# A graph layer's row gathers: one tile in 88 fetched by SP row by row, in place of a GpSimd gather

## The chip, the cores and the metric

The kernel runs on one core of a Trainium2 chip. A core has TensorE (matmuls, "PE" in the profile, its weight loads "PEld"), VectorE ("DVE"), ScalarE ("ACT"), GpSimd ("POOL") and SyncE ("SP"), an on-chip memory of 128 partitions (SBUF), accumulators for TensorE (PSUM), and DMA engines that move data between the chip's main memory and SBUF. SP here only issues transfers. Times are device microseconds of one launch; the number compared is the median of several launches.

## What is computed

A layer of a graph network, all in float32: 12,500 nodes with 96 features, 412,500 edges sorted by target node, 4 features an edge.

```
node    = mlp(x, W_node)                        # mlp: relu(h @ W + b), then a batch norm over the rows
edge    = mlp(edge_attr, W_edge)
message = mlp([x[src], x[dst], edge], W_msg)    # 412,500 rows
agg     = segment_sum(message, dst)
out     = layernorm(x + agg + node)
```

The product with W_msg is split by its three parts. `x @ W_msg[0]` and `x @ W_msg[1]` are made once for all nodes and stand in main memory as the tables `p_tab` and `q_tab`. For an edge the kernel then needs the row `src` of `p_tab` and the row `dst` of `q_tab`. Since edges are sorted by `dst`, rows of `q_tab` come as short windows; rows of `p_tab` lie anywhere and have to be gathered, 384 bytes each.

## The kernel before

A tile is 128 edges, a group (`GT`) four tiles, a block (`BG`) four groups. There are 806 groups in 202 blocks. `gather` (L162) fetches one group of `p_tab` rows by four indirect transfers on GpSimd, one for each tile: the edge numbers in `src` choose the row that lands on each of 128 partitions.

The first 26 blocks ("early", the constant `SPILL`) are gathered while the tables, the node part and the edges' statistics are still being computed, and are parked in main memory (`spill`). Gathers of later groups go to a ring of 25 slots in SBUF (`RING`, tile `pg`), which is filled before the long stage starts. In the long stage (L502 to L534) one step k handles one group. Steps run over the late blocks with the early ones spread evenly among them. For each step:

- at the first group of a block, `load(s + 2)` has SP fetch the edge features (L396) and the edges' relative targets (L397) for two blocks at once, then read the block's first target into a register (L400) and fetch the window of `q_tab` with that address (L405); `fetch(s + 1)` has SP read a parked block back (L412);
- `linear(k + 1)` has TensorE compute z, the target and edge part of the next group (L452);
- `message(k)` has VectorE add z and the gathered rows (`hs`, L467) and ScalarE apply relu (L469). This addition is the last reader of the ring slot;
- `sums(k - 2)` has TensorE multiply the messages by the 0/1 matrix of their targets and by themselves (L484), for the sums and for the statistics; `edges` (L437), `prepare` (L444, L445) and `add` (L497, L498) serve whole blocks;
- if the step's group was a late one, `ahead_of(ahead)` takes the slot just freed and gathers the group 25 places further on.

The order of instructions on all five engines in this stage is the order written (`manual_schedule`); waits between engines are put in by the framework. Each engine works its list in order, so an SP instruction that waits holds back everything SP issues after it. Landings of SP's transfers are counted on a few counters that take turns; a transfer waits until the one before it on the same counter has landed.

Of the kernel before, what the change touches and what calls it, by code (L numbers as in the profile page):

```python
# [11 lines left out]
F32 = mybir.dt.float32  # L12
I32 = mybir.dt.int32
# [3 lines left out]
ET = mybir.EngineType  # L17
# [3 lines left out]
N, C, E, ED = 12500, 96, 412500, 4  # L21
EPS = 1e-5
P = 128
# [3 lines left out]
GT, GE, BG = 4, 512, 4  # L27
NT = -(-E // P)
NG = -(-NT // GT)
NBL = -(-NG // BG)  # L30
NTP, NGP = NBL * BG * GT, NBL * BG
EP = NGP * GE
# [21 lines left out]
KR = C + WN + 1  # L54

SPILL = 26 * BG
RING = 25
RAW = 3
SKEW = 6
HB, RB = 2, 3  # L60
CL, CE = 2, 2
J = 8


# [12 lines left out]
def gnn(ctx, tc, t):  # L77
    nc = tc.nc
    const = ctx.enter_context(tc.tile_pool(name="const", bufs=1))
    dram = ctx.enter_context(tc.tile_pool(name="dram", bufs=1, space=DRAM))  # L80
    p_tab = dram.tile([NN, C], F32, name="p_tab")
# [10 lines left out]
    nc.sync.dma_start(src_raw, t["src"][:, :RAW * BG * GT])  # L92
    ring = rpool.enter_context(tc.tile_pool(name="ring", bufs=RING))
    xp = xpool.enter_context(tc.tile_pool(name="x", bufs=1)).tile([C, XW], F32, name="xp")
# [64 lines left out]
            queues[c // CH % len(queues)].dma_start(rows[:, c:c + CH, :], r)  # L159
            yield  # L160

    def gather(g, pg):  # L162
        tab, idx = (t["x"], src_raw) if g < RAW * BG else (p_tab, src)
        for i in range(min(GT, NT - g * GT)):
            k = g * GT + i
            nc.gpsimd.indirect_dma_start(  # L166
                out=pg[:, i, :], out_offset=None, in_=tab[:, :],
                in_offset=bass.IndirectOffsetOnAxis(ap=idx[:, k:k + 1], axis=0))
        return pg
# [107 lines left out]
    def edge_norm():  # L277

        with tc.tile_pool(name="es", bufs=2) as work, tc.tile_pool(name="es1", bufs=1) as one, \
                tc.tile_pool(name="es_ps", bufs=4, space=PSUM) as ps:  # L280
            stats = one.tile([P, NS, NBL, 6], F32, name="estats")
            for b in range(NBL):
                if b % J == 0:
                    yield
                    ea = work.tile([P, J, GE], F32, name="ea")
                    n = min(J, NBL - b)
                    for i in range(NS):
                        nc.sync.dma_start(ea[Q * i:Q * i + 2 * EK, :n, :],
                                          t["ea"][EK * i:EK * (i + 2), b:b + n, :])
                for i in range(NS):  # L290
                    k = NS * b + i
                    if k % 2 == 0:
                        pr = ps.tile([P, 2, GE], F32, name="pr")
                    nc.tensor.matmul(pr[:, k % 2, :], wide[Q * i:Q * i + 2 * EK, :],  # L294
                                     ea[Q * i:Q * i + 2 * EK, b % J, :], start=True, stop=True)
                    if k % 2:
# [32 lines left out]
            nc.vector.tensor_scalar(w_e, w_msg[:, 2, :], a_e, None, op0=OP.mult)  # L329

    def fast(ring):
        def ahead_of(g):
            return gather(g, ring.tile([P, GT, C], F32, name="pg"))

        with tc.manual_schedule(engines={ET.SP, ET.Pool}):
            with tc.tile_pool(name="tab_w", bufs=1) as work, tc.tile_pool(name="tab_ps", bufs=2, space=PSUM) as ps:
# [18 lines left out]
            for _ in store:  # L355
                pass
            got = {g: ahead_of(g) for g in range(SPILL, SPILL + RING)}

# [10 lines left out]
        with tc.tile_pool(name="fix", bufs=1) as fix, tc.tile_pool(name="msg", bufs=2) as work, \  # L369
# [17 lines left out]
            def load(s):  # L387

                b = order[s]
                first = SPILL // BG  # L390
                c, o = ((b - first) // CL * CL + first, CL) if b >= first else (b // CE * CE, CE)
                if c not in eas:
                    o = min(o, NBL - c)
                    eas[c] = work.tile([P, o, GE], F32, name="ea" if b >= first else "eae")
                    for i in range(BG):
                        nc.sync.dma_start(eas[c][Q * i:Q * i + EK, :, :], t["ea"][EK * i:EK * (i + 1), c:c + o, :])  # L396
                    nc.sync.dma_start(eas[c][EK:P:Q, :, :], rel_d[:, c * BG * GE:(c + o) * BG * GE]  # L397
                                      .rearrange("o (b g e) -> (o g) b e", g=BG, e=GE))
                ea = eas[c][:, b - c, :]
                _, val = nc.values_load_multi_w_load_instructions(  # L400
                    base[:, b:b + 1], engines=[ET.SP], min_val=0, max_val=N - 1,
                    skip_runtime_bounds_check_because="they are nodes' numbers")
                rows = q_tab[bass.ds(val[0], WN), :]
                rows = bass.AP(rows.tensor, rows.offset, [[C, WN], [WS * C, BG], [1, C]], None, rows.runtime_checks)
                nc.sync.dma_start(rhs[C:C + WN, s % RB, :, :], rows)  # L405
                block[s] = ea

            def fetch(s):
                b = order[s]
                if b * BG < SPILL:  # L410
                    back = work.tile([P, BG, GT, C], F32, name="pb")
                    nc.sync.dma_start(back, spill[b].rearrange("p g (a c) -> p g a c", a=GT))  # L412
                    for i in range(BG):
                        got[b * BG + i] = back[:, i, :, :]
# [18 lines left out]
            def edges(s):  # L433

                prs[s] = ps.tile([P, BG, GE], F32, name="pr", bufs=1)
                for i in range(min(BG, NG - order[s] * BG)):
                    nc.tensor.matmul(prs[s][:C + WN, i, :], we[Q * i:Q * i + EK + 1, :],  # L437
                                     block[s][Q * i:Q * i + EK + 1, :], start=True, stop=True)

            def prepare(s):  # L440

                n = min(BG, NG - order[s] * BG)
                pr, x = prs[s], left[s % 2]
                nc.scalar.activation(x[:C, :n, :], pr[:C, :n, :], AF.Relu)  # L444
                nc.vector.tensor_scalar(x[C:C + WN, :n, :], pr[C:C + WN, :n, :], 0.0, None, op0=OP.is_equal)  # L445

            def linear(k):
                s, g = steps[k]
                n = min(GT, NT - g * GT)
                zs[k] = ps.tile([P, GT, C], F32, name="z")  # L450
                for i in range(n):
                    nc.tensor.matmul(zs[k][:, i, :], left[s % 2][:KR, g % BG, i * P:(i + 1) * P],  # L452
                                     rhs[:KR, s % RB, g % BG, :], start=True, stop=True)

            def message(k):
                s, g = steps[k]
                n = min(GT, NT - g * GT)
                i = g % BG
                h, z, pg = hb[s % HB], zs.pop(k), got.pop(g)
                if i == 0:  # L460
                    nc.vector.tensor_tensor(  # L461
                        h[:, :, :, C + 1:C + 1 + WN], rel[:, g:g + BG, :].unsqueeze(3).to_broadcast([P, BG, GT, WN]),
                        iota.unsqueeze(2).to_broadcast([P, BG, GT, WN]), op=OP.is_equal)
                if i % 2 == 0:
                    pair[0] = work.tile([P, 2, GT, C], F32, name="hs")
                hs = pair[0]
                nc.vector.tensor_add(hs[:, i % 2, :n, :], z[:, :n, :], pg[:, :n, :])  # L467
                if i % 2 and n == GT:
                    nc.scalar.activation(h[:, i - 1:i + 1, :, :C], hs, AF.Relu)  # L469
                elif i % 2 or g == NG - 1:  # L470
                    for o in range(i // 2 * 2, i + 1):
                        m = GT if o < i else n
                        nc.scalar.activation(h[:, o, :m, :C], hs[:, o % 2, :m, :], AF.Relu)
# [13 lines left out]
            def add(s):  # L487
# [9 lines left out]
                    nc.vector.tensor_tensor(to, pa[:, i:n:2, C + 1:C + 1 + WN], to, op=OP.add)  # L497
                nc.vector.tensor_add(gram[:, :n, :], pa[:, :n, :C + 1], gram[:, :n, :])  # L498

            n, ahead = len(steps), SPILL + RING  # L502
            with tc.manual_schedule(engines={ET.SP, ET.Pool, ET.PE, ET.DVE, ET.Activation}):
                load(0)
                fetch(0)
                load(1)
                edges(0)
                prepare(0)
                linear(0)
                for k in range(n + SKEW):  # L510
                    s, g = steps[min(k, n - 1)]
                    if k < n and g % BG == 0:
                        if s + 2 < len(order):
                            load(s + 2)
                        if s + 1 < len(order):
                            fetch(s + 1)
                    if k + 1 < n:
                        linear(k + 1)
                    if k < n:
                        message(k)  # L520
                    if 0 <= k - 2 < n:
                        sums(k - 2)
                    if k < n and s + 1 < len(order):
                        if g % BG == 0:
                            edges(s + 1)
                        if g % BG == 2:
                            prepare(s + 1)
                        if g % BG == 3 and order[s + 1] < RAW:
                            convert(s + 1)
                    if k >= SKEW and (k - SKEW) % BG == 0:  # L530
                        add((k - SKEW) // BG)
                    if k < n and g >= SPILL and ahead < NG:
                        got[ahead] = ahead_of(ahead)
                        ahead += 1  # L534

            d = fix.tile([C, BG, C], F32, name="d")
            s = fix.tile([C, 3], F32, name="s")
# [237 lines left out]
```

## Time and profile before

| | |
|---|---|
| median of 3 launches | 5365.1 us (5362.86 to 5375.22) |
| the profiled execution's own time | 5383.6 us |
| its span, first to last instruction | 5381.9 us |
| busy in the span: TensorE, VectorE, ScalarE, GpSimd | 3389.5, 1708.3, 1077.3, 3088.7 us |
| mean granted TensorE clock | 0.662 of full |
| gathers on GpSimd into the ring | 2807, mean 958 ns |
| main memory traffic | 50 GB/s over the span |

A row of instructions gives the source line, the engine, what is written and read, the count, the busy time, the mean duration of one, and then the engine's idle time just before these instructions and what ended most of it. "issue" there means that the profile shows no wait, "remote" that it can't name who ended the wait. A row of waits gives who waited for whom, the total in us, the number of times and the longest. SPq rows are SP's own list: its durations are those of issuing.

### The profile page before, as it was taken

What the parts mean: (1) busy time and instruction counts of PE and PEld (TensorE: products, weight loads), DVE (VectorE), ACT (ScalarE), POOL (GpSimd) and SP (SyncE); (2) the same over time, 40 slices, a digit from 0 to 9 for tenths busy, and PEclk for the clock granted to TensorE, in tenths of its full rate; (3) what the DMA queues carried; (4) which work ended last, traced back from release to release, by engine and by line L of the source; (5) the groups of instructions that cost most, each with busy time, mean ns of one, the idle gap of its engine ahead of it and who ended that gap; (6) DMA issues with size and microseconds to landing.
All of it is one profiled execution on the core that took longest, in us unless ns stands there. A gap on an engine that the chain in (4) does not pass through costs nothing. (4 is left out here: it accounts for less than half of the span.)

```text
span 5381.9 us, 46696 instructions
## 1 busy us (share of the span) xinstructions
PE 3389.5 (63%) x16705; PEld 2576.6 (48%) x16705; DVE 1708.3 (32%) x2635; ACT 1077.3 (20%) x1015; POOL 3088.7 (57%) x3231
## 2 busy tenths in 40 slices
PE   5557653566666666666666666666666666765668
PEld 5423321354545555445554445454555544554557
DVE  1446542622222222223222223222232223222225
ACT  0235432311111111111111111111111111111112
POOL 5553455255566666666666665666666666666660
PEclk9755555566766666666676676666666666667667
DMA  5333322111111111111111111111111111111112
GB/s 165 127 87 66 71 62 50 27 37 33 39 44 37 43 43 43 44 37 43 43 43 41 45 36 43 43 42 44 37 43 42 42 45 36 43 43 42 45 36 83
DMA packets 154401, 270.78 MB, mean 50 GB/s; under 512 B 83463, under 2 KB 83976, under 8 KB 153154
## 3 DMA queue, kind: packets, MB, share of 16 engines
q0 software_dynamic: 103136, 158.62, 13.8%
q1 hardware_dynamic: 47936, 98.39, 6.4%
q10 hardware_dynamic: 3088, 10.71, 0.6%
q8 instruction: 133, 2.18, 0.2%
q14 instruction: 108, 0.88, 0.1%
HBM read 225.88 MB, written 41.60 MB: 50 GB/s over the span
## 5 line engine op out<-in xcount | busy, mean ns | idle before, releaser
L166 POOL DMA_INDIRECT pg<-p_tab,src x2807 | 2689.2, 958 | 1785.6 <-DVE hs L467 953.3
L452 PE MATMUL z<-rhs,left 128*128 128x96 f32 x6446 | 1221.4, 337 | 886.4 <-issue 766.5
L452 PEld LDWEIGHTS z<-rhs,left 128*128 128x128 f32 x6446 | 1094.8, 248 | 1181.1 <-issue 987.6
L484 PE MATMUL pa<-h 128*97 128x128 f32 x6446 | 1241.8, 331 | 522.8 <-issue 519.7
L484 PEld LDWEIGHTS pa<-h 128*97 128x97 f32 x6446 | 1012.0, 209 | 628.3 <-issue 626.2
L467 DVE TENSOR_TENSOR hs<-z,pg 128x384 f32<-128x384 f32 x702 | 384.7, 555 | 2634.4 <-remote 1730.7
L469 ACT ACTIVATE h<-hs 128x768 f32<-128x768 f32 x402 | 339.7, 845 | 2891.3 <-DVE hs L467 1768.6
L294 PE MATMUL pr<-ea,wide 10*128 10x512 f32 x1212 | 403.1, 1074 | 296.3 <-issue 197.6
L166 POOL DMA_INDIRECT stage<-p_tab,src x368 | 352.9, 959 | 355.8 <-DMA spill<-stage 224.6
L437 PE MATMUL pr<-ea,we 6*127 6x512 f32 x1404 | 458.7, 856 | 80.9 <-issue 67.9
L444 ACT ACTIVATE left<-pr 96x2048 f32<-96x2048 f32 x202 | 377.2, 1867 | 641.5 <-remote 452.0
L445 DVE TENSOR_SCALAR left<-pr 31x2048 f32<-31x2048 f32 x202 | 462.8, 2291 | 130.7 <-ACT left L444 84.2
L300 DVE BATCH_NORM_STATS2 estats<-r 128x6 f32<-128x512 f32 x606 | 365.5, 701 | 333.9 <-issue 217.8
L294 PEld LDWEIGHTS pr<-ea,wide 10*128 10x128 f32 x1212 | 203.3, 321 | 494.8 <-issue 316.3
L298 ACT ACTIVATE r<-pr 128x1024 f32<-128x1024 f32 x303 | 296.3, 1026 | 459.2 <-remote 261.4
L437 PEld LDWEIGHTS pr<-ea,we 6*127 6x127 f32 x1404 | 133.4, 235 | 255.1 <-issue 241.8
L461 DVE TENSOR_TENSOR h<-rel,iota 128x496 f32<-128x496 f32 x202 | 134.8, 667 | 0.0
L154 PE MATMUL pt<-w_msg,xp 96*128 96x96 f32 x392 | 89.3, 422 | 61.8 <-issue 38.5
L497 DVE TENSOR_TENSOR agg<-pa,agg 97x62 f32 x404 | 90.1, 223 | 105.0 <-remote 78.8
L154 PEld LDWEIGHTS pt<-w_msg,xp 96*128 96x128 f32 x392 | 85.5, 330 | 65.4 <-issue 50.6
L467 DVE TENSOR_TENSOR hs<-z,pb 128x384 f32<-128x384 f32 x104 | 57.2, 554 | 177.7 <-PE z L452 82.4
L498 DVE TENSOR_TENSOR gram<-pa,gram 97x388 f32<-97x388 f32 x202 | 111.4, 551 | 0.0
(107 smaller groups left out, 611.5 us busy)
## 6 DMA issues: line engine op xcount, KB each, us to landing
pg<-p_tab,src POOLq DMA_INDIRECT x2807
spill<-stage SPq DMA_DIRECT2D x26, 768.0 KB
pb<-spill SPq DMA_DIRECT2D x26, 768.0 KB
ea<-in_ea SPq DMA_DIRECT2D x75, 160.0 KB
rhs<-q_tab SPq DMA_DIRECT2D x202, 46.5 KB
ea<-in_ea SPq DMA_DIRECT2D x352, 20.0 KB
stage<-p_tab,src POOLq DMA_INDIRECT x368
q_tab<-trow SPq DMA_DIRECT2D x7, 672.0 KB
```

The costliest lines, as they stand in the source:

```text
L154: nc.tensor.matmul(pt[:, g, :], xp[:, k:k + P], w, start=True, stop=True)
L166: nc.gpsimd.indirect_dma_start(out=pg[:, i, :], out_offset=None, in_=tab[:, :], in_offset=bass.IndirectOffsetOnAxis(ap=idx[:, k:k + 1], ax ...
L294: nc.tensor.matmul(pr[:, k % 2, :], wide[Q * i:Q * i + 2 * EK, :], ea[Q * i:Q * i + 2 * EK, b % J, :], start=True, stop=True)
L298: nc.scalar.activation(r, pr, AF.Relu)
L300: nc.vector.bn_stats(stats[:, (k - o) % NS, (k - o) // NS, :], r[:, 1 - o, :])
L437: nc.tensor.matmul(prs[s][:C + WN, i, :], we[Q * i:Q * i + EK + 1, :], block[s][Q * i:Q * i + EK + 1, :], start=True, stop=True)
L444: nc.scalar.activation(x[:C, :n, :], pr[:C, :n, :], AF.Relu)
L445: nc.vector.tensor_scalar(x[C:C + WN, :n, :], pr[C:C + WN, :n, :], 0.0, None, op0=OP.is_equal)
L452: nc.tensor.matmul(zs[k][:, i, :], left[s % 2][:KR, g % BG, i * P:(i + 1) * P], rhs[:KR, s % RB, g % BG, :], start=True, stop=True)
L467: nc.vector.tensor_add(hs[:, i % 2, :n, :], z[:, :n, :], pg[:, :n, :])
L469: nc.scalar.activation(h[:, i - 1:i + 1, :, :C], hs, AF.Relu)
L484: nc.tensor.matmul(pas[s][:, g % BG, :C + 1 + WN], h[:r, i, :C + 1], h[:r, i, :C + 1 + WN], start=i == 0, stop=i == n - 1)
```

## The change

The ring has 24 slots. Of every 22 groups (`SG`) that are gathered ahead in the long stage, one is marked `by_row`: GpSimd gathers three of its four tiles, and SP fetches the fourth, one row at a time. A list of its 128 row numbers (a new input, `rows`) is brought into one partition by one small transfer, 22 groups earlier. At every second group (`SS`) SP loads twelve (`SR`) of these numbers into registers and issues twelve transfers of one row each, from `p_tab` at the register's address to one partition of the slot. Eleven such batches make the tile. A group is marked if at least 22 groups are left from it on.

```diff
-RING = 25
+RING = 24
+SR, SS = 12, 2
+SG = SS * -(-P // SR)
...
-    def gather(g, pg):
+    def gather(g, pg, without=0):
         tab, idx = (t["x"], src_raw) if g < RAW * BG else (p_tab, src)
-        for i in range(min(GT, NT - g * GT)):
+        for i in range(min(GT, NT - g * GT) - without):
...
+            def row_numbers(g):
+                lin = work.tile([1, P], I32, name="lin")
+                nc.sync.dma_start(lin, t["rows"][g * GT + GT - 1:g * GT + GT, :])
+                return lin
+
+            def rows_of(pg, lin, lo, hi):
+                _, val = nc.values_load_multi_w_load_instructions(
+                    lin[:, lo:hi], engines=[ET.SP], min_val=0, max_val=N - 1,
+                    skip_runtime_bounds_check_because="they are nodes' numbers")
+                for p in range(lo, hi):
+                    nc.sync.dma_start(pg[p:p + 1, GT - 1, :], p_tab[bass.ds(val[p - lo], 1), :])
...
             n, ahead = len(steps), SPILL + RING
+            lins = {ahead: row_numbers(ahead)}
...
                     if k < n and g >= SPILL and ahead < NG:
-                        got[ahead] = ahead_of(ahead)
+                        m = (ahead - SPILL - RING) % SG
+                        if m == 0:
+                            by_row = ahead if ahead + SG <= NG else None
+                        got[ahead] = ahead_of(ahead, int(ahead == by_row))
+                        if by_row is not None and m % SS == 0:
+                            if m == 0 and ahead + 2 * SG <= NG:
+                                lins[ahead + SG] = row_numbers(ahead + SG)
+                            lo = m // SS * SR
+                            rows_of(got[by_row], lins[by_row], lo, min(lo + SR, P))
                         ahead += 1
```

`ahead_of` passes `without` on to `gather`.

More of the change, by code (lines that the diff above doesn't have):

```diff
@@ L331, in fast, with ahead_of @@
     def fast(ring):
-        def ahead_of(g):
-            return gather(g, ring.tile([P, GT, C], F32, name="pg"))
+        def ahead_of(g, without=0):
+            return gather(g, ring.tile([P, GT, C], F32, name="pg"), without)
         with tc.manual_schedule(engines={ET.SP, ET.Pool}):
@@ L749 @@
     give("src", np.pad(s, (0, EP - E)).reshape(NTP, P).T)
+    give("rows", np.pad(s, (0, EP - E)).reshape(NTP, P))
     give("dst", d.reshape(NTP, P).T)
```

## The prediction

> **What bounds the kernel now.** I read the groups of instructions first, then the waits of GpSimd and of SP, then the order of time inside the long stage (from 1033 us, where the gathers go on, to 5250 us, where the last one ends).
>
> ```profile
> span 5381.9 us, 46696 instructions
> L166 POOL DMA_INDIRECT pg<-p_tab,src x2807 | 2689.2, 958 | 1785.6 <-DVE hs L467 953.3
> L452 PE MATMUL z<-rhs,left 128*128 128x96 f32 x6446 | 1221.4, 337 | 886.4 <-issue 766.5
> L467 DVE TENSOR_TENSOR hs<-z,pg 128x384 f32<-128x384 f32 x702 | 384.7, 555 | 2634.4 <-remote 1730.7
> ```
>
> No engine is full. One gather costs 0.95 us and 0.30 us to the next, 1.25 us in all, 5.0 us for a group of four. GpSimd's waits:
>
> ```profile
> POOL pg L166 <- DVE hs L467: 953.3, 175, 132.5
> POOL pg L166 <- issue: 785.0, 2477, 3.0
> ```
>
> It gathers in bursts, and each burst ends when the ring has no free slot, until an addition on L467 frees one. In the gather records of the stage I count 157 waits of 1 to 6 us (564 us, 3.6 each), 25 longer ones (286 us, where groups from the spill are consumed) and 3367 us of gathering: together 4217 us for 677 groups, 6.23 us a group; a burst has 4.3 groups. So the stage is the time of the gathers plus a gap after each burst. Why the ring runs out shows in order of time (start, length, engine, count, idle before):
>
> ```profile
> 3020.01 0.56 DVE L467 TENSOR_TENSOR hs<-z,pg 128x384 f32<-128x384 f32 x1 [6.86 <-PE pr L437]
> ...
> 3024.93 1.03 PE L452 MATMUL z<-rhs,left 128*128 128x96 f32 x3 [1.08 <-issue]
> 3029.28 0.94 POOL L166 DMA_INDIRECT pg<-p_tab,src  x1 [0.30 <-issue]
> ...
> 3033.44 1.02 DVE L467 TENSOR_TENSOR hs<-z,pg 128x384 f32<-128x384 f32 x2 [12.87 <-remote]
> 3034.15 1.92 PE L452 MATMUL z<-rhs,left 128*128 128x96 f32 x8
> 3034.27 0.94 POOL L166 DMA_INDIRECT pg<-p_tab,src  x1 [4.04 <-DVE hs L467]
> ```
>
> From 3016 to 3033 TensorE advances by about one instruction in 0.70 us, waiting for nothing shown; three microseconds after GpSimd stops it does eight in 1.9 us again. I call this the slow mode. Ten to fifteen microseconds after a burst begins it sets in, and it ends with the burst: I find 1545 us of it in the stage, 2.28 us a group. Three windows of 3.6 us, two slow and one fast (columns: TensorE busy and its instructions, weight loads and theirs, and so on):
>
> ```profile
> 2139.00:2142.60 3.60, 0.76 (x3) 0.48 (x3) 0.00 (x0) 0.00 (x0) 2.84 (x3) 0.50 0.23 52
> 3050.80:3054.40 3.60, 0.73 (x4) 0.71 (x4) 0.00 (x0) 0.82 (x1) 2.84 (x3) 0.71 0.19 41
> 3128.00:3131.60 3.60, 3.60 (x33) 2.79 (x31) 1.92 (x4) 1.69 (x2) 1.66 (x2) 1.00 0.14 37
> ```
>
> SP is hit too, which matters here: in the first of them, its register instructions on L405 took 697 and 709 ns; outside the slow mode they take 37, 17 and 29. VectorE's stay at 50 to 100 ns in both.
>
> **The change part by part.** *Removed from GpSimd:* one gather in 88. The first by-row group is 128, the last one must leave 22 groups behind it, so there are 30; 30 x 1.25 = 37 us, which lies in bursts and so on the path. *Ring 24 for 25:* one group less is gathered ahead of the stage (5 us more inside it) and one less is left after the last gather (85 us for about 25 groups, 3.4 us less): 2 us. The lead of a gather over its use, about 140 us, falls by 6, and hides the rest.
>
> *Added to SP:* 30 x 128 = 3840 transfers of 384 B, each with an address calculation and a register move before it, 330 loads of row numbers, 30 loads of a list. The trace has these instructions:
>
> ```profile
> L377 SPq DMA_DIRECT2D rhs<-bias x12: 581/589/609, 1012.5 to 1019.5; - x12
> L405 SPq FUSED_REGOPS  x202: 3/37/707, 1022.9 to 5284.3; - x101
> L405 SPq MOVE rhs<-q_tab x202: 2/29/1387, 1023.0 to 5284.4; - x101
> L405 SPq DMA_DIRECT2D rhs<-q_tab x202: 258/290/780, 1023.0 to 5292.7; - x101
> ```
>
> L377 is the nearest row: one partition, 384 B, 0.63 us from one to the next. With 0.09 and 0.06 for the two register instructions a row costs 0.78 us; by the issue of L405 (31 partitions, 0.34 from one to the next) it would be 0.49. I take 0.78, as the one-partition transfer is the same shape. Here the Trainium skill's rule can be weighed ("DMA: Bandwidth & Descriptors", section "Latency and other measured facts"): a tiny transfer can't be faster than about 0.8 us. Over SP's eight landing counters, which each row transfer must find free, that would be an estimated 0.1 us a row, 13 us a tile: hidden, and the sum would be the bare 35 us gained. By the row of the trace SP's own issue is what counts: 128 x 0.78 = 100 us a tile. The same page's section "Issuing engines are not separate DMA queues" says that issuing from more engines saves only the sequencer's time, usually small; here that time (1.25 us a gather) is just what is on the path, so it sets no lower price.
>
> *SP's day.* Per gathered group, at full speed: 128/22 = 5.8 rows x 0.78 = 4.5 us; a load of row numbers every second group (0.75 us by L400's records) 0.4; the old loads of a block (L396, L397, L400, L405, about 2.3 us a block, 1.15 blocks per four groups) 0.7. Sum 5.6 us of the 6.23 us that a group lasts. That would fit, but for the slow mode: three instructions at 0.70 us make a row at least 2.1 us, so 1 us of slow mode does 0.37 us of SP's work. What a group then needs is 5.6 + 0.63 x 2.28 = 7.0 us, 0.8 us over what there is: +520 us over 677 groups, if the slow mode keeps its length. It doesn't quite: when SP is late, TensorE or VectorE stands, GpSimd fills its ring sooner and stops, the slow mode ends early and SP runs fast. With none of the loss left the slow mode would have to be 1.0 us a group. I take 1.65, between them: 5.6 + 1.04 = 6.64, 0.41 x 677 = +278 us, in which the 35 us of GpSimd are no longer on the path. SP's waits for TensorE (L405) fill its idle time now; rows that overlap them are free, so I round down to +225.
>
> *Who waits behind SP.* Its queue is in order. A late batch of twelve holds back the next block's L396 and L397 (about two blocks of slack, 45 us), L405 (two blocks), the read from the spill on L412 (one block, 22 us). L405 late stops L452; L412 late stops L467. The last batch of a tile is issued 20 of the ring's 24 groups after the first, so it has 4 groups, some 25 us, before L467 needs it; eight rows in slow mode take 17 us or more. The first row of a tile waits for L467 to free the slot, which SP's present waits already match. VectorE gets 104 more waits of 0.1 us, GpSimd 119 of 0.02 us before gathers: 10 and 2 us, in idle time.
>
> *TensorE itself.* In the 58 clearest fast windows it gets through about 135 instructions and weight loads before the slow mode; fitted over these, each SP instruction in the window goes with 0.8 fewer (standard error 0.4). If SP's rows use up the same allowance, the slow mode comes sooner. I don't add it, as it acts on the same stretches; it raises the upper end.
>
> The profile's own time is 5383.6 us about a span of 5381.9, the median 5365.1; I add the differences to the median: 5365 + 225 = 5590.
>
> **The rivals.**
> - *SP keeps up: faster.* A row must cost 0.61 us or less (5.8 c + 1.1 + 2.28 (1 - c/2.1) = 6.23). L405's own 0.34 us issue speaks for it, L377's 0.63 against. Then 37 - 2 = 35 us are gained: 5330. Chance 0.17.
> - *Near the balance:* SP is late now and then and eats the gain, 5349 to 5381. Chance 0.06.
> - *SP is late, slow mode shortened* (the forecast): 5400 to 5740 about 5590. Chance 0.57.
> - *SP is late and the slow mode keeps its length, or the rows bring it on sooner:* +450 to +600 us, 5815 to 5965. For it: the fit above; against it: a stopped GpSimd ends the mode each time. Chance 0.20.
> - That the change doesn't do what it says is excluded: SP's stream has 3840 row transfers more, GpSimd's 30 gathers fewer.
>
> **How the numbers follow.** A difference under 0.3% (16 us) can't be told from none here. Faster 0.17, same 0.06, slower 0.77. The range goes from the first rival's 5330 to 5840, the lower part of the last: it leaves out about half of each, 0.18. The forecast's own range is 5400 to 5740.
>
> **What would show it.** Right: row transfers near 0.6 us each and two or three times that in bursts; SP waiting on L405 no longer 3100 us but a small part of it; L452 or L467 waiting for what SP brought; more time in GpSimd's gaps. Wrong: if rows take 0.35 us, or if SP's slow instructions are rare although rows are issued in bursts, SP keeps up, and the time is 5330.

## The result, and the profile after

The changed kernel takes 5660.3 us (median of 4 launches, 5653.5 to 5662.3), the kernel before 5368.7 us beside it (5362.9 to 5375.2): a ratio of 1.055, interval 1.053 to 1.057. The change costs 5.5%, 292 us. The forecast was 5590 us.

Line numbers of the changed kernel are two higher up to the stage's loop: L166 is now L168, L405 is L407, L452 is L454, L467 is L469. The rows are L513. First the page of the changed kernel: the span, then groups of instructions (busy time, mean ns, idle before and what ended most of it).

```profile
span 5651.8 us, 58871 instructions
...
L168 POOL DMA_INDIRECT pg<-p_tab,src x2777 | 2659.3, 958 | 2083.1 <-DVE hs L469 1176.2
L454 PE MATMUL z<-rhs,left 128*128 128x96 f32 x6446 | 1246.6, 351 | 1032.4 <-issue 609.2
...
L469 DVE TENSOR_TENSOR hs<-z,pg 128x384 f32<-128x384 f32 x702 | 385.3, 554 | 2216.7 <-remote 1058.6
```

GpSimd has 30 gathers fewer, each still costs 958 ns, and it is busy 30 us less. Its idle time is 298 us more, 2083.1 for 1785.6. Counted in its records as for the prediction, and over the same 677 groups, the stage now lasts from 1033 to 5519 us: 174 gaps of 1 to 6 us with 624 us (before 157 with 564), 36 longer ones with 543 us (before 25 with 286), and the gathering itself takes some 50 us less. The stage is 269 us longer, and the rest of the program (133 us after the last gather, 132 before) is as it was.

What fills the longer gaps shows in the waits. First SP's own list in the kernel before and then in the changed one (who waits for whom, total us, times, longest):

```profile
SPq L405 <- remote: 1893.5, 94, 32.1
SPq L405 <- PE z L452: 1252.5, 78, 31.4
```

```profile
SPq L407 <- PE z L454: 101.8, 10, 19.1
...
SPq L513 <- DMA pg<-p_tab: 64.6, 106, 1.4
SPq L407 <- remote: 51.8, 8, 25.8
```

SP used to stand 3146 us at the load of the `q_tab` window. The program has it wait there until TensorE has done with an older window; the profile names TensorE for 1252.5 us of it and can't name the releaser of the rest. It now stands there 154 us: nearly all of that time is spent on rows. Then who waits for what SP brings, first in the kernel before, then in the changed one:

```profile
PE pr L437 <- DMA ea<-rel_d: 11.9, 1, 11.9
```

```profile
DVE hs L469 <- DMA pb<-spill: 225.6, 17, 24.4
...
DVE hs L469 <- DMA pg<-p_tab: 95.9, 8, 20.1
...
PE pr L439 <- DMA ea<-rel_d: 81.8, 16, 17.0
...
DVE hs L469 <- DMA lin<-in_rows: 77.9, 8, 18.1
...
DVE hs L469 <- DMA ea<-in_ea: 57.9, 3, 22.6
```

In the kernel before, that one wait of 11.9 us is the only one for these blocks' loads that is over 1 us. Here VectorE and TensorE stand still for parked blocks, edge features and targets, all of which SP issues behind its rows, and in a smaller part for rows of the tile itself. (The additions on L469 don't read `lin`; that wait was for something else late on the same counter.)

These waits lie where the time was lost. Inside GpSimd's gaps of the stage (850 us before, 1168 now) VectorE's idle time that ends with a transfer of SP's is 0 us before and 266 us now. Its idle time there that "remote" ended is the same (389 and 380 us), and so is, within 25 us, that for TensorE's z.

The rows themselves, in the records of L513 (count, ns shortest/median/longest, first and last start):

```profile
L513 SPq FUSED_REGOPS  x3840: 2/37/1409, 1027.3 to 5417.0; - x192
L513 SPq MOVE pg<-p_tab x3840: 1/29/1402, 1027.6 to 5417.0; - x192
L513 SPq DMA_DIRECT2D pg<-p_tab x3840: 2/225/1538, 1027.9 to 5417.7; - x192
```

The medians add up to 0.29 us, and undisturbed rows follow each other at 0.41 us. But each of the three can take 0.7 or 1.4 us. Of the 3510 steps from one row's issue to the next inside batches, 1825 are short (688 us in all), and 1685 are 0.6 us or longer, here called stretched (2471 us, mean 1.47): 3159 us together, 0.90 a row. In order of time (start, length, engine, count) the stretch that answers to the one shown of before, with SP in it:

```profile
3012.06 1.13 POOL L168 DMA_INDIRECT pg<-p_tab,src  x1 [4.53 <-DVE hs L469]
...
3014.27 0.27 SPq L407 DMA_DIRECT2D rhs<-q_tab  x1
...
3015.75 23.46 SPq L513 DMA_DIRECT2D pg<-p_tab  x24
...
3029.09 0.37 PE L486 MATMUL pa<-h 128*97 128x128 f32 x1 [1.82 <-issue]
...
3034.82 0.56 DVE L469 TENSOR_TENSOR hs<-z,pg 128x384 f32<-128x384 f32 x1 [1.96 <-remote]
...
3035.65 1.13 POOL L168 DMA_INDIRECT pg<-p_tab,src  x1 [3.71 <-DVE hs L469]
...
3039.95 0.00 SPq L407 DMA_DIRECT2D rhs<-q_tab  x1
3041.05 3.18 SPq L513 DMA_DIRECT2D pg<-p_tab  x4
```

GpSimd's burst starts at 3012 and ends at 3032. From 3015.8 to 3039.2 SP issues 24 rows and nothing else of weight, and only then the next block's window load. By its single records, its first rows follow each other at 0.41 us, the stretching begins at 3018, from 3022 to 3034.7 a row takes 2.1 us and more, and then 0.41 again. TensorE falls to one instruction in 0.70 us at about 3026, eight microseconds after SP.

### The profile page after: what moved, and what is told of

Its sections match the earlier page's. It is cut to its first block, busy times and chain, and to the rows that moved or that the text cites. A ratio compares the mean times of both kernels' runs of the same rounds, so it can differ in the third digit from the quotient of the medians.

```text
span 5651.8 us, 58871 instructions
## 1 busy us (share of the span) xinstructions
PE 3307.7 (59%) x16705; PEld 2619.6 (46%) x16705; DVE 1703.8 (30%) x2635; ACT 1074.3 (19%) x1015; POOL 3060.3 (54%) x3201
## 3 DMA queue, kind: packets, MB, share of 16 engines
q14 instruction: 204, 1.67, 0.1%
## 5 line engine op out<-in xcount | busy, mean ns | idle before, releaser
L168 POOL DMA_INDIRECT pg<-p_tab,src x2777 | 2659.3, 958 | 2083.1 <-DVE hs L469 1176.2
L454 PE MATMUL z<-rhs,left 128*128 128x96 f32 x6446 | 1246.6, 351 | 1032.4 <-issue 609.2
L454 PEld LDWEIGHTS z<-rhs,left 128*128 128x128 f32 x6446 | 1127.9, 260 | 1371.0 <-issue 888.2
L486 PE MATMUL pa<-h 128*97 128x128 f32 x6446 | 1282.9, 342 | 626.5 <-issue 625.0
L486 PEld LDWEIGHTS pa<-h 128*97 128x97 f32 x6446 | 1068.9, 220 | 679.7 <-issue 678.0
L469 DVE TENSOR_TENSOR hs<-z,pg 128x384 f32<-128x384 f32 x702 | 385.3, 554 | 2216.7 <-remote 1058.6
L168 POOL DMA_INDIRECT stage<-p_tab,src x368 | 354.4, 963 | 354.6 <-DMA spill<-stage 221.5
L439 PE MATMUL pr<-ea,we 6*127 6x512 f32 x1404 | 306.0, 873 | 119.7 <-DMA ea<-rel_d 81.8
L439 PEld LDWEIGHTS pr<-ea,we 6*127 6x127 f32 x1404 | 82.8, 246 | 180.1 <-issue 138.3
L469 DVE TENSOR_TENSOR hs<-z,pb 128x384 f32<-128x384 f32 x104 | 56.0, 553 | 346.3 <-DMA pb<-spill 225.6
```

The costliest lines, as they stand in the source:

```text
L168: nc.gpsimd.indirect_dma_start(out=pg[:, i, :], out_offset=None, in_=tab[:, :], in_offset=bass.IndirectOffsetOnAxis(ap=idx[:, k:k + 1], ax ...
L486: nc.tensor.matmul(pas[s][:, g % BG, :C + 1 + WN], h[:r, i, :C + 1], h[:r, i, :C + 1 + WN], start=i == 0, stop=i == n - 1)
```

## The experiments

Two groups of runs have to be told apart. The slow mode was there when the result and the first four runs were taken, and the kernel before takes 5368.7 and 5362.3 us beside them. In the three sessions after that (launches taken together) it was absent for every kernel, and the kernel before takes 4165 us. The first four runs and the next four, a quarter of an hour later, have the same chip number, 12; the last have 4 and 0. So each ratio is against the kernel before in the same session.

### With the slow mode (kernel before 5362.3 us)

**scratch12.** GpSimd gathers all four tiles of every group. SP still fetches the 3840 rows, into a spare tile that nobody reads. The output is the full one.

```diff
-                        got[ahead] = ahead_of(ahead, int(ahead == by_row))
+                        got[ahead] = ahead_of(ahead)
...
-                            rows_of(got[by_row], lins[by_row], lo, min(lo + SR, P))
+                            rows_of(spare, lins[by_row], lo, min(lo + SR, P))
```

> GpSimd gathers all four tiles of every group again; SP issues the same 3840 row transfers in the same places, into a spare tile that nobody reads. Theory (SP's list is full: slow-mode stretches make its rows last about 0.95 us on average, so the loads behind them come late): the loss stays, less what waits for the rows themselves, and the 37 us of gathers come back on top where GpSimd sets the pace: 5600 to 5700 us. Rival A (VectorE waits for a tile whose rows land late): no reader, so the loss goes: 5365 to 5390 us. Rival B (the rows use up TensorE's allowance before the slow mode): the loss stays, 5600 to 5700, and the half dose tells it from the theory.

Measured 5714.4 us, 1.066 (1.062 to 1.070), 14 us over the expected range. The loss is all there, 352 us, though no row can be late for anyone. It is 60 us more than the changed kernel's (47 by the profiled spans). The waits of this kernel:

```profile
DVE hs L469 <- DMA pb<-spill: 325.4, 21, 20.1
...
PE pr L439 <- DMA ea<-rel_d: 112.2, 24, 11.9
...
PE pr L439 <- DMA eae<-rel_d: 44.1, 7, 16.2
```

What is late is the blocks' own loads, which stand behind the rows in SP's list. GpSimd's gaps are as long as in the changed kernel (1169 us), and VectorE's idle time in them that ends with a transfer of SP's is 240 us, 214 of it for parked blocks. GpSimd's gathering takes 41 us more than in the changed kernel, so the 30 gathers that come back do lengthen the stage here.

**scratch6.** The same as scratch12 with six rows a batch, so 66 rows of each of the 30 tiles, 1980 in all.

```diff
-                            lo = m // SS * SR
-                            rows_of(spare, lins[by_row], lo, min(lo + SR, P))
+                            lo = m // SS * (SR // 2)
+                            rows_of(spare, lins[by_row], lo, min(lo + SR // 2, P))
```

> As the spare-tile kernel, but six rows a batch in place of twelve (half the row transfers, nobody reads them, GpSimd gathers everything). Theory (a list that is either full or not): SP has about 1760 us of rows in a stage of 4220 where it stood idle for 3600, so it keeps up: 5365 to 5430 us, SP waiting on its window load for well over 1000 us. Rival B (each SP instruction takes a share of an allowance): half the loss, 5480 to 5540 us.

Measured 5398.2 us, 1.0075 (1.005 to 1.010): 36 us, a tenth of scratch12's loss for half its rows. SP still waits for TensorE:

```profile
SPq L407 <- remote: 1258.1, 155, 23.0
SPq L407 <- PE z L454: 361.1, 40, 26.7
```

and neither `pb` nor `ea` nor `rel_d` makes anyone wait more than in the kernel before (11.9 us, once); inside GpSimd's gaps (864 us) VectorE waits 0 us for SP's transfers. So the price is not per row. It begins where SP's spare time ends. The balance can be worked out from SP's records of the stage, each time counted from one instruction's start to the next:

| us in the stage | before | scratch6 | changed | scratch12 |
|---|---|---|---|---|
| rows | 0 | 1422 | 3430 | 3481 |
| register loads of row numbers | 0 | 409 | 303 | 290 |
| from the register move of a window load to its issue | 3637 | 1641 | 176 | 174 |
| span of the program, against before | | +14 | +270 | +317 |

The third row is SP's spare time: for all 195 window loads it is 3637 us in the kernel before, where the view of the waits finds 3146 us in 172 of them. In scratch6 nearly half of it is left. In the changed kernel and in scratch12 rows and register loads take 3733 and 3771 us, more than the 3637 there are, so the stage has to grow. It grows by more than that difference, since SP is not late everywhere: 176 and 174 us of spare time are still left.

**act12.** The change, with the registers and the rows on ScalarE.

```diff
-                    lin[:, lo:hi], engines=[ET.SP], min_val=0, max_val=N - 1,
+                    lin[:, lo:hi], engines=[ET.Activation], min_val=0, max_val=N - 1,
...
-                    nc.sync.dma_start(pg[p:p + 1, GT - 1, :], p_tab[bass.ds(val[p - lo], 1), :])
+                    nc.scalar.dma_start(pg[p:p + 1, GT - 1, :], p_tab[bass.ds(val[p - lo], 1), :])
```

> The change as it is, but registers and row transfers are ScalarE's instead of SP's, twelve at a time in the same places. Theory (what hurts is SP's in-order list in the slow mode; ScalarE's instructions were not stretched in the trace of before): the loss goes, unless five microseconds of issuing in front of ScalarE's own work hold TensorE up: 5330 to 5450 us, row spacing near 0.41 us throughout. Rival C (the small transfers themselves, on the DMA engines or in memory, are what costs): 5600 us or more, whoever issues them. If ScalarE is stretched as well: 5700 us and more.

Measured 5530.6 us, 1.030 (1.026 to 1.034): 168 us lost in place of 292, between the ranges expected. The same 3840 transfers cost less from another engine, so the transfers as such can't be all of the 292. I had supposed that only TensorE and SP are slowed. ScalarE's rows are stretched too (0.86 us from one issue to the next inside batches):

```profile
L513 ACTq FUSED_REGOPS  x3840: 2/37/1397, 1026.9 to 5307.8; - x192
...
PE pa L486 <- ACT h L471: 473.6, 127, 14.6
```

The second line is the form that the loss seems to take here: the relu stands behind a batch of rows, and the matmuls of `sums` behind the relu. In the kernel before, no matmul of `sums` waits for ScalarE.

**ring24.** The kernel before with a ring of 24.

```diff
-RING = 25
+RING = 24
```

> Before with 24 ring slots instead of 25, nothing else. Theory: 0 to 5 us slower, 5365 to 5375 us. If the ring's length sets how long the gaps are: 25 us slower or more.

Measured 5361.0 us, 1.0002 (0.9988 to 1.0015). The smaller ring costs nothing that shows.

### Without the slow mode (kernel before 4166.4, 4164.6 and 4165.0 us)

The expected times of scratch9, loads_act, scratch12_loads_act and split were written for a kernel before at about 5362 us, and so stand on the wrong level.

**after_again.** The changed kernel, without an edit.

> The changed kernel, unedited, to see it where the slow mode is absent: in the last four runs the kernel before took 4166 us on the same chip, with no stretch in which TensorE or SP is stretched, and GpSimd gathering without a gap. Theory (SP's list is full only because of the slow mode; a row costs 0.41 us outside it): if the slow mode is absent again, SP needs about 60 of the 109 us that 22 groups last and keeps up, and the gathers saved are 30 x 1.24 = 37 us of GpSimd's gapless list: 4120 to 4140 us beside 4166 for before. If the slow mode is there again: 5650 to 5670 beside 5365. Rival (rows cost by themselves): slower than before in both.

Measured 4116.9 us (4113.9 to 4119.7) against 4164.6, 0.989 (0.987 to 0.990), 3 us under the expected range: the change *gains* 48 us. Its page, waits and records of L513:

```profile
span 4112.9 us, 58871 instructions
...
L168 POOL DMA_INDIRECT pg<-p_tab,src x2777 | 2643.7, 952 | 847.1 <-issue 695.1
...
L469 DVE TENSOR_TENSOR hs<-z,pg 128x384 f32<-128x384 f32 x702 | 389.7, 555 | 1975.5 <-DMA pg<-p_tab,src 1648.1
```

```profile
SPq L407 <- PE z L454: 583.7, 87, 19.7
```

```profile
L513 SPq FUSED_REGOPS  x3840: 37/37/42, 648.0 to 3840.6; - x192
...
L513 SPq DMA_DIRECT2D pg<-p_tab x3840: 221/228/287, 648.3 to 3840.8; - x192
```

The address calculation never takes more than 42 ns, where it took up to 1409, and TensorE's pattern is gone as well: from one of its instructions to the next there are 0.65 to 0.75 us 813 times in the changed kernel's stage with the slow mode, and 4 times here. SP still has time to wait for TensorE. GpSimd has no gap over 1 us in the whole stage, and VectorE waits for its gathers 1648 us: the gathers are the bound here. A gather costs this kernel 1.249 us from one to the next, so 30 fewer are 37.5 us.

**scratch9.** The spare-tile kernel with nine rows a batch.

```diff
-                            lo = m // SS * SR
-                            rows_of(spare, lins[by_row], lo, min(lo + SR, P))
+                            lo = m // SS * 9
+                            rows_of(spare, lins[by_row], lo, min(lo + 9, P))
```

> Spare-tile kernel with nine rows a batch (30 x 99 rows, nobody reads them, GpSimd gathers everything). Theory (SP's list is full or not): nine rows need about 2600 to 2700 us of SP plus 600 of loads in the stage, just short of full, with queues behind bad stretches: 5420 to 5520 us, SP's wait on its window load a few hundred us. A loss in proportion to rows (from 36 us at six and 352 at twelve there is none such) would give 5540.

Measured 4164.4 us, 0.9996 (0.9989 to 1.0003). 2970 rows that bring nothing cost nothing, so the question for which it was made (where between six and twelve the loss begins) wasn't answered. As it is the kernel before in all but rows that don't matter, its profile can stand beside that of after_again. Its last gather ends at 4095.2 us, that of after_again at 4044.2, and the spans differ by the same, 4163.8 against 4112.9. The 51 us are 30 gathers (37.5 us) and 13 us of prolonged steps: over the whole program, gathers that start over 1.4 us after the one before are 115 in scratch9 and 91 in after_again, with 65.8 and 52.6 us over the usual step.

**loads_act.** The kernel before, with the blocks' loads (features, targets, window, parked block) issued by ScalarE, so that SP's list is nearly empty. The edit is the same on five lines:

```diff
-                nc.sync.dma_start(rhs[C:C + WN, s % RB, :, :], rows)
+                nc.scalar.dma_start(rhs[C:C + WN, s % RB, :, :], rows)
```

> Control for the next one: before, with the block loads (edge features, targets, first target's register, window, parked block) issued by ScalarE instead of SP; no rows. Theory: 5355 to 5400 us.

Measured 4138.3 us, 0.9935 (0.9915 to 0.9956), 28 us gained; **loads_act_again**, the same kernel in the last session:

> The kernel before with the blocks' own loads issued by ScalarE, beside the one above. If the kernel before takes about 5362 us: ScalarE's loads are stretched as SP's are (its transfers were in the run with the rows on ScalarE), but they are only about 5 instructions a block, so 5350-5400; if ScalarE's relu is held up by them, 5400-5500. If the kernel before takes about 4165 us: 4138 us again, within 5.

4140.2 us, 0.9937 (0.9920 to 0.9953). In the first of the two, prolonged steps of GpSimd add up to 37.5 us, 28 less than in scratch9, which is the gain. Why GpSimd's steps are longer when SP issues these loads, no run here shows.

**scratch12_loads_act.** Twelve rows a batch by SP into the spare tile, the blocks' loads by ScalarE.

> The spare-tile kernel with twelve rows a batch, SP full as before, but the block loads are ScalarE's, so nothing waits for SP any more. Theory (the cost is that the loads stand behind the rows in SP's list): close to the control, 0 to 60 us above it. Rival (rows cost by themselves: memory, DMA engines, or an allowance that TensorE shares): the 352 us stay, 5650 to 5750 us.

Measured 4143.5 us, 0.9949 (0.993 to 0.997): against loads_act, 3840 rows cost 5 us, and each kernel's launches spread over 7 or 8 us. Whether the loss goes when no load stands behind a row is not shown by it, as there was no loss.

**split.** The change, with six rows of each batch on SP and six on ScalarE.

```diff
-                _, val = nc.values_load_multi_w_load_instructions(
-                    lin[:, lo:hi], engines=[ET.SP], min_val=0, max_val=N - 1,
+                for queue, engine, lo, hi in ((nc.sync, ET.SP, lo, (lo + hi) // 2),
+                                              (nc.scalar, ET.Activation, (lo + hi) // 2, hi)):
+                  _, val = nc.values_load_multi_w_load_instructions(
+                    lin[:, lo:hi], engines=[engine], min_val=0, max_val=N - 1,
```

> The change, with each batch's first six rows issued by SP and the other six by ScalarE. Theory: SP has room at six rows (36 us lost in the spare-tile kernel), ScalarE loses less than half of what twelve cost it; 37 us of gathers are saved: 5370 to 5440 us. If the two lists don't share a limit and slack covers both: 5330 to 5350 us.

Measured 4114.0 us, 0.9876 (0.9858 to 0.9894), and **split_again**:

> Six rows of each batch on SP, six on ScalarE. If the kernel before takes about 5362 us: six rows on SP alone cost 36 us and twelve on ScalarE 168, so by the knee seen with six rows, SP keeps up and ScalarE's half costs little: 5370-5450; if the stretched instructions of both engines add up as one budget, 5500-5660. If the kernel before takes about 4165 us: 4114 us again, within 5.

4112.7 us, 0.9872 (0.9855 to 0.9888): the change's gain, and no more.

**after_loads_act.** The changed kernel with the blocks' loads on ScalarE, the edits of loads_act on it. With the slow mode it would have been the test of the queued loads.

> The changed kernel with the blocks' own loads issued by ScalarE, so that SP's list holds only the lists and the rows. If the kernel before takes about 5362 us (TensorE and SP at times at 0.70 us an instruction): my theory is that the loss is the blocks' loads queued behind stretched rows in SP's list; with them on another engine only the late end of a tile can hold VectorE, and the time falls from 5660 us to 5370-5480; the rival, that the stretched rows themselves or more of the slow mode are the loss, 5580-5700. If the kernel before takes about 4165 us: GpSimd's gapless list sets the end; the change's 37 us and the 28 us of this move add up if each shortens different steps: 4090-4105; if they shorten the same prolonged steps (the accounting put 11 us of the change's 48 on those), 4105-4118.

Measured 4109.7 us, 0.986 (0.985 to 0.988). The two gains, 48 and 28 us, don't add up: together they are 55 us. Its prolonged steps come to 49.5 us, only 3 less than those of after_again. Its interval overlaps that of after_again and of split, so it is the fastest measured here by a little at most. With the slow mode none of these versions was run, and there nothing measured beats the kernel before.

## Why the prediction was right, and where it was wrong

The sign and the mechanism came out: SP fills up, the blocks' loads behind its rows come late, and GpSimd's gaps grow. So did the size, 292 us for the 225 forecast, inside the forecast's own range (5400 to 5740); but that was luck, as two terms of the sum were wrong in opposite directions. Step by step:

- *30 gathers removed, 37 us; ring, 2 us.* Right without the slow mode: 37.5 us where GpSimd is the bound; and nothing for the ring. That with SP late they would be off the path looks wrong: scratch12, which has the rows and these gathers too, has the same gaps and 41 us more of gathering.
- *What bounds the stage.* Right with the slow mode: gathers plus gaps. The time came in as longer gaps (from 850 to 1168 us, the filling of the ring left out), and not as dearer gathers.
- *A row at 0.78 us.* Wrong. This is the step that failed. The one-partition copy of L377 was taken as the nearest row, because it has the same shape. The transfer alone takes 0.23 us, not 0.59, and a row 0.41 us undisturbed. The issue of L405, whose address also comes from a register and whose source is also main memory, was nearer (0.34, and 0.49 with the register work). The estimate of 0.1 us a row that the prediction worked out from the Trainium skill ("DMA: Bandwidth & Descriptors", "Latency and other measured facts") was too low, at a quarter of the undisturbed 0.41: SP's own issue was the price, as the row of the trace had it, only at half the size. The page's least time of about 0.8 us for one transfer is not tested by any run here.
- *Slow mode costs SP 0.63 of its time, for 1.65 us a group.* Wrong, the other way. TensorE's pattern of one instruction in 0.70 us lasts 1131 us in this stage, 1.67 us a group, just as assumed. But SP is stretched more often than TensorE. Of its 2471 us in stretched steps only some 650 lie where TensorE shows the pattern; for about 1000 TensorE's instructions follow each other within 0.5 us. Counted from the start of a gather burst, a row takes 0.59 us on average in the first 5 us, 1.24 in the next 5, 2.01 from 10 to 15, and 2.58 from 15 to 20. I had SP slowed from 10 to 15 us on.
- *The sum, 6.64 us a group.* It is 6.63 (4486 us for 677 groups), but by two errors that cancel. Rows were to take 4.5 us and the slowing to add 1.04, together 5.5; the rows' 3430 us of the stage are 5.07 a group, of which only 1.02 are short steps. Register loads take 0.45, SP's spare time 0.26, and the old loads the remaining 0.85. With a row at its true 0.41 us and the slowing as I had it, the prediction's own condition for "SP keeps up" (0.61 or less) would have held, and the forecast would have been 5330.
- *The median.* 5660 is 70 above the forecast; the profiled span gives 270 us of loss, the medians 292, and I had rounded 278 down to 225 for rows that overlap waits. That allowance was one too many: SP's idle time at the window load had already been spent in the balance.
- *What waits behind SP.* Right. The largest part is the parked blocks (225.6 of the 515 us that VectorE waits for SP's transfers in the stage), which have the least slack, one block, as said.
- *Rows start the slow mode sooner on TensorE.* Not seen. In bursts of over 12 us TensorE's pattern (two steps in a row of 0.6 to 1.5 us) begins a median 13.4 us after the burst's start in the kernel before, 12.9 in the changed one, and 13.5 and 14.3 in scratch6 and scratch12.
- *The slow mode keeps its length.* It doesn't, as said: 1545 us of it before, 1131 after, and 1086 and 1194 in scratch6 and scratch12. (The absolute figures hang on how the pattern is counted. Taking all stretches of four matmul steps that average 0.5 to 1.0 us, it is 1532, 1187, 1043 and 1255.) With the full length, 5815 to 5965 were due.
- *The length of a burst.* The prediction's 4.3 groups leave out the 25 longer gaps; over all 182 gaps it is 3.7. Nothing in the sum rests on it.
- *SP keeps up: faster.* This rival is what happens without the slow mode: 35 us said, 48 measured, of which 37.5 are the gathers. Its condition holds there, with 0.43 us on average from one row's issue to the next inside batches.

That the slow mode would be there was taken from the trace and never doubted; it is the largest condition of the whole forecast. The prediction asked for "row transfers near 0.6 us" and called 0.35 the sign that SP keeps up. The undisturbed rows were nearer to the second, and the time still went up, since it is the stretched half that fills SP.

What stays open: what switches the slow mode on; and the direct test of the loss (blocks' loads on another engine while the mode is there), which no run made. That the queued loads are the loss rests on VectorE's waits for them inside GpSimd's gaps in the changed kernel and in scratch12, on their absence in scratch6, and on SP's balance.

## What to carry to other kernels

An engine that only issues transfers has a budget as any other has: add up its issue time at the mean it will have beside the work around it, not at its median, and compare that with its present idle time. Below that the work was nearly free here (36 us for 1980 rows), above it everything queued behind pays, first the load with the least slack. And before a tuned kernel's stage is costed from one trace, see whether the same kernel has the same time in another session: here the same change costs 292 us in one and gains 48 us in another.

## What was not expected of the hardware

- The slow mode belongs neither to the kernel nor, it seems, to the chip: 5362 and 4166 us for the same kernel, on chips of the same number, a quarter of an hour apart. Within a session the launches of the kernel before lie within 0.9%. The mean granted clock goes with it, 0.662 and about 0.74. Whether it is cause or effect is not shown; single instructions of 37 ns that take 0.7 or 1.4 us are no matter of a clock that falls by a tenth.
- It reaches ScalarE as well when ScalarE issues transfers from register addresses (act12), and it reaches SP sooner than TensorE: in the changed kernel the first stretched row comes a median 2.8 us after a burst's start, TensorE's pattern 12.9. VectorE's address calculations never take more than 104 ns in either kernel's stage. And with the rows on ScalarE, SP's own register instructions on the window load are hardly stretched any more (1 of 390 over 0.6 us; 46 of 390 before). Why is not shown.
- A transfer of one 384-byte row from main memory, at a register's address, is issued in 0.23 us, and 0.41 us after the one before; the copy of 384 bytes within SBUF that I took for its like needs 0.59.
- Moving the blocks' loads (three to four transfers a block) from SP to ScalarE took 28 us off GpSimd's prolonged steps (65.8 in scratch9, 37.5 in loads_act). What links the two is not shown.
